# Moving the query stage's normalisations, transposes and two small bias steps in a two-layer attention and feed-forward kernel

## The chip, the cores and the metric

The kernel runs on one core of one Trainium2 chip. A core has engines that run side by side and meet only at semaphores: TensorE (PE in the profile; its weight loads are PEld), VectorE (DVE), ScalarE (ACT), GpSimd (POOL) and SyncE (SP), which here issues most of the transfers between memory and the on-chip buffer. The metric is device microseconds for the whole program; each time given for the kernel is a median over runs.

## The reference: what is computed

Inputs are `x` (8 batches of 112 tokens, width 512), a context `ctx` (8 batches of 375 rows, width 512) and masks of valid context rows, all float32. Two layers follow each other, each an attention over the context and a feed-forward net of hidden size 1408, and all four parts add their result to `x`:

```
x = x + xattn0(layernorm(x), ctx, mask)          # one head, softmax(x ctx^T / sqrt(512)) ctx
x = x + ffn0(layernorm(x), w1, w2, w3)           # quantized: activations to 8 bits, weights to -1, 0, 1
x = x + xattn1(layernorm(x), ctx, mask, Wq, bq, Wk, bk, Wv, bv, Wo, bo, ln_gamma, ln_beta, residual_scale)
x = x + ffn1(layernorm(x), wq_gate, s_gate, wq_up, s_up, wq_down, s_down)
```

The change touches the second attention, cut to what matters here (16 heads of 32):

```
q = hs @ Wq.T + bq;  k = at @ Wk.T + bk;  v = at @ Wv.T + bv        # hs = layernorm(x), at = ctx
scores = clip(q k^T / sqrt(32), -50, 50), masked;  probs = softmax(scores)
ctx = probs @ v
delta = clip(residual_scale, 0, 0.3) * (ctx @ Wo.T + bo)
return layernorm(delta) * ln_gamma + ln_beta
```

Since the probabilities of a row sum to 1, the bias of the values reaches the output as a constant, `bv @ Wo.T`. The kernel computes the values without it and adds that constant to `bo`.

## The kernel before, in words

**Tiles.** The 896 tokens are 7 tiles of 128 rows (`xs[0]` to `xs[6]`, slices of `tokens`). Products run over tokens in two groups: group 0 is tiles 0 to 3, group 1 tiles 4 to 6 (`GROUPS`). "Turning" a tile is transposing it on TensorE against an identity matrix, into PSUM, from where ScalarE or VectorE copies it.

**Stages.** First the attention of layer 0, one batch at a time (about 0 to 100 us), then its feed-forward net, one tile at a time (to about 218 us), the queries of layer 1 (to 244 us), its attention in 8 batches of 3 context chunks (to some 413 us) and its feed-forward net. Through all of these until near the end, `fill(n)` takes the next n steps of `key_value_steps`, which compute keys and values of layer 1 (L193, L202) as work for TensorE in between.

**What sets the order.** TensorE and SP run in the order in which the program is written. Inside `written` (from the middle of layer 0's attention to L694) and in the attention of layer 1 (`work2`) all five engines do. Between the two, which is the stretch of the queries, and in the first microseconds, a planner orders VectorE, ScalarE and POOL by its own estimate of durations. It can also place such free instructions among those of `written`. A buffer is handed on when all readers of its former tile are done.

**Preparing the queries.** For each tile, `write2` (L217) normalises it on VectorE into a tile `d` of two buffers (L644 for tiles 0 to 3, L156 for tiles 4 to 6). `transpose2` (L221) turns it with four transposes (L226) into a PSUM tile `s` of a pool of four buffers. Then ScalarE writes a rounded high part (L229); the function that `transpose2` returns, the tile's "end", has VectorE write the low part (L232, which reads PSUM) and a difference (L233). `turn_down0(6)` turns the last tile of layer 0's net: 11 transposes (L349) into two more buffers of `s`, each copied by ScalarE (L351). In the kernel before, tiles 0 and 1 are turned, then for each of them its end and the write of tile 2 or 3 follow, then `turn_down0(6)`, the turning of tiles 2 and 3, their ends, one step of `fill` (L202) and the last down product (L579, added to `xs[6]` in L581).

**The queries.** `queries(g)` (L724) goes over four chunks of 128 columns: 8 products (L732, L734) of high and low parts, 4 more (L738) of the difference into a second PSUM tile `less`, from the `s` pool; ScalarE adds the queries' bias `bq` (L740) and VectorE subtracts `less` (L742) into `qT`. Ahead of them POOL issues loads (L163): bq, wo, bo, gamma, beta, rs, the mask m, later sg and su. L711 and L713 work on rs. `normaliser` computes a tile's statistics (L143, L144) and a chain of small VectorE operations (L152, L121 to L133): "ln2b" for tiles 4 and 5, "ln2c" for tile 6. On TensorE, two chunks of group 0 come first, then tiles 4, 5 and 6 are turned with one chunk after each as long as there are some (two), then group 1's four chunks.

**The values' bias.** `fold_bias` (L745) is a generator of two steps: four VectorE operations over Wo, scaled by bv (L748, L750), and a product with ones (L754) added to bo (L755). It is run around group 1's queries. Its result is first used when a tile is projected (L804), in batch 2.

**The attention of layer 1.** For each batch b and context chunk c: scores on TensorE (L900), clipped on VectorE (L905), exponentials on ScalarE (L906), a step of `fill`, and the products with the values and the row sums (L926, L921) of the chunk before. POOL adds up exponentials (L892) and converts weights (L877).

Of the kernel before, what the change touches and what calls it, by code (L numbers as in the profile page):

```python
# [23 lines left out]
F32 = mybir.dt.float32  # L24
# [11 lines left out]
P = 128  # L36
B, T, D = 8, 112, 512
KC = D // P
# [4 lines left out]
NT = B * T // P  # L43
# [27 lines left out]
def two_layers(ctx: ExitStack, tc: tile.TileContext, x, ctxT, ctxN, mask0, mask1, w1, w2, w3,  # L71
               wq, wk, wv, wo, bq, bk, bv, bo, gamma, beta, rscale,
               wg, sg, wu, su, wd, sd, out):
    nc = tc.nc
# [5 lines left out]
    kvp = kvs.enter_context(tc.tile_pool(name="kvp", bufs=1))  # L80
# [16 lines left out]
    xs = [tokens[:, i, :] for i in range(NT)]  # L97
# [49 lines left out]
    def normaliser(srcs, name):  # L147

        mv = moments(srcs, name)
        r = srcs[0].shape[0]  # L150
        ve = small[-1].tile([P, len(srcs)], F32, name=f"{name}_ve", bufs=1)[:r]
        nc.vector.tensor_scalar_add(ve, mv[:, :, 1], LN_EPS)  # L152
        rstd = rsqrt(ve, name)

        def write(h, j):
            nc.vector.tensor_scalar(h, srcs[j], mv[:, j, 0:1], rstd[:, j:j + 1],  # L156
                                    ALU.subtract, ALU.mult)
        return write


    def load(pool, src, shape, name, queue=nc.sync, dtype=F32):
        t = pool.tile(shape, dtype, name=name)
        queue.dma_start(out=t, in_=src)  # L163
        return t

    bk_s = kvp.tile([P, KC], F32, name="bk")
    bv_s = kvp.tile([P, KC], F32, name="bv")
    wk_s = kvp.tile([P, KC, D], F32, name="wk")
    wv_s = kvp.tile([P, KC, D], F32, name="wv")
# [40 lines left out]
    def fill(n=1):  # L210
        for _ in range(n):
            next(kv_steps, None)
# [4 lines left out]
    def write2(i, write, j, pool):  # L217
        h2[i] = pool.tile([P, D], F32, name="d", bufs=2)
        write(h2[i], j)

    def transpose2(i, psum):  # L221

        g = 0 if i < GROUPS[0][1] else 1
        pt = psum.tile([P, KC, P], F32, name="s")
        for kc in range(KC):
            nc.tensor.transpose(pt[:, kc, :], h2[i][:, kc * P:(kc + 1) * P], ident)  # L226
        j = i - GROUPS[g][0]
        high, low, diff = (t[:, :, j * P:(j + 1) * P] for t in h2T[g])
        nc.scalar.activation(high, pt, AF.Identity, scale=LESS)  # L229

        def end():
            nc.vector.tensor_sub(low, pt, high.bitcast(F32))  # L232
            nc.vector.scalar_tensor_tensor(diff, high.bitcast(F32), SPLIT, low.bitcast(F32),  # L233
                                           ALU.mult, ALU.subtract)
        return end


    with tc.tile_pool(name="w0", bufs=1, side="right") as w0p, \
# [119 lines left out]
        with tc.tile_pool(name="work0", bufs=2, side="right") as work0, \  # L358
                tc.tile_pool(name="last0", bufs=1, side="right") as last0:

            m0 = load(work0, mask0, [B, S2], "m0", nc.scalar, U8)
            nc.scalar.dma_start(out=bk_s, in_=bk)
            x0 = []
            LN0 = (0, 1, 4)
            cNs, normal, h0, hT0, s0, eT0 = {}, {}, {}, {}, {}, {}
# [162 lines left out]
        with tc.tile_pool(name="work1", bufs=2, side="right") as work1:  # L528
# [43 lines left out]
            def turn_down0(i):  # L572
                q3[i] = transposed_h(q3[i][0], H, "q3", work1), q3[i][1]
# [45 lines left out]
            for i in range(2, NT):  # L619
# [61 lines left out]
                elif i == 5:  # L681
                    wq_diff = []
                    h2T_diff = difference()
                    h2T[0] = h2T_high, difference(), h2T_diff
            ends = [transpose2(k, ps_s) for k in range(2)]
            for k in range(2):
                ends[k]()
                write2(k + 2, normal2, k + 2, work1)
            turn_down0(NT - 1)
            ends = [transpose2(k, ps_s) for k in range(2, 4)]  # L690
            for end in ends:
                end()
            fill(1)
            written.close()  # L694
# [4 lines left out]
    tailp = ctx.enter_context(tc.tile_pool(name="tailp", bufs=1, side="right"))  # L699

    ps_s = ctx.enter_context(tc.tile_pool(name="ps_s1", bufs=4, space=PSUM))
    ps_mm = ctx.enter_context(tc.tile_pool(name="ps_mm1", bufs=2, space=PSUM))
    kv_psum[0] = ps_mm

    bq_s = load(tailp, bq, [P, KC], "bq", nc.gpsimd)
    wo_s = load(tailp, wo, [P, KC, D], "wo", nc.gpsimd)
    bo_s = load(tailp, bo.to_broadcast([P, D]), [P, D], "bo", nc.gpsimd)
    gamma_s = load(tailp, gamma.to_broadcast([P, D]), [P, D], "gamma", nc.gpsimd)
# [15 lines left out]
    def queries(g):  # L724
        i0, i1 = GROUPS[g]
        cols = slice(i0 * P, i1 * P)
        high, low, diff = h2T[g]
        for dc in range(KC):
            of = slice(dc * P, (dc + 1) * P)
            ps = ps_mm.tile([P, 512], F32, name="mm")[:, :(i1 - i0) * P]  # L730
            for kc in range(KC):
                nc.tensor.matmul(ps, lhsT=wq_high[:, kc, of], rhs=high[:, kc, :],  # L732
                                 start=(kc == 0), stop=False)
                nc.tensor.matmul(ps, lhsT=wq_low[:, kc, of], rhs=low[:, kc, :],  # L734
                                 start=False, stop=(kc == KC - 1))
            less = ps_s.tile([P, 512], F32, name="s")[:, :(i1 - i0) * P]
            for kc in range(KC):
                nc.tensor.matmul(less, lhsT=wq_diff[kc // 2][:, kc % 2, of], rhs=diff[:, kc, :],  # L738
                                 start=(kc == 0), stop=(kc == KC - 1))
            nc.scalar.activation(qT[:, dc, cols], ps, AF.Identity, bias=bq_s[:, dc:dc + 1],  # L740
                                 scale=1.0 + SPLIT)
            nc.vector.tensor_sub(qT[:, dc, cols], qT[:, dc, cols], less)  # L742
            yield

    def fold_bias():  # L745

        t = tailp.tile([P, D], F32, name="d", bufs=2)
        nc.vector.tensor_scalar_mul(t, wo_s[:, 0, :], bv_s[:, 0:1])  # L748
        for kc in range(1, KC):
            nc.vector.scalar_tensor_tensor(t, wo_s[:, kc, :], bv_s[:, kc:kc + 1], t,  # L750
                                           ALU.mult, ALU.add)
        yield
        ps = ps_mm.tile([P, D], F32, name="mm")
        nc.tensor.matmul(ps, lhsT=ones, rhs=t, start=True, stop=True)  # L754
        nc.vector.tensor_add(bo_s, ps, bo_s)  # L755
        yield

    kv_psum[1] = False
    asking = queries(0)
    next(asking)  # L760
    next(asking)
    with tc.tile_pool(name="g1p", bufs=1, side="right") as g1p:
        h2T[1] = [g1p.tile([P, KC, 384], F32R, name=f"h2T1_{k}") for k in range(3)]
        write = normaliser(xs[4:6], "ln2b")
        for i in range(4, NT):
            if i == NT - 1:
                write = normaliser(xs[i:], "ln2c")
            write2(i, write, i % 2, tailp)
            transpose2(i, ps_s)()
            next(asking, None)  # L770
        folding = fold_bias()
        next(folding)
        for _ in queries(1):
            pass
        next(folding)
    queried.close()
    tail2 = ctx.enter_context(tc.tile_pool(name="tail2", bufs=1, side="right"))

# [67 lines left out]
    with tc.tile_pool(name="work2", bufs=1, side="right") as work2, \  # L846
# [95 lines left out]
        STEPS = [3, 3, 3, 3, 2, 3, 3, 3]  # L942
        ADD_POOL = range(B - 1)
        last, rdens, later = None, {}, []
        counts = list(due.values())
        load_integers(counts.pop(0))
        for b in range(B):
            for c in range(NCK):
                if c == 2 and b in ADD_POOL:
                    add(b)  # L950
                if (b, c) in due:
                    convert_integers()
                    if counts:
                        load_integers(counts.pop(0))
                es = scores(b, c)
                if c == 2 and b not in ADD_POOL:
                    add(b)
                if c < STEPS[b]:
                    fill(1)
                if c == NCK - 1:  # L960
                    sums(*last)
                if (b, c) == (B - 1, NCK - 1):
                    over = tailp.tile([P, 29], F32, name="over")
                    nc.gpsimd.tensor_scalar(over, squares, WIDE, 1.0, ALU.is_gt, ALU.mult)
                if c == 0:
                    while later:
                        later.pop()()
                    if b >= 3:
                        project_end(b - 3)
                elif c == 1 and b >= 1:  # L970
                    divide(b - 1)
                elif c == 2:
                    turned = 3 <= b < 3 + GROUPS[0][1]
                    if turned:
                        write4(b - 3)
                    if b >= 2:
                        project_product(b - 2)
                    if b == B - 1:

                        hits = ps_s.tile([1, 29], F32, name="s")  # L980
                        nc.tensor.matmul(hits, lhsT=ones[:, :1], rhs=over, start=True, stop=True)
                        wide = tailp.tile([1, 1], I32, name="wide")
                        nc.vector.tensor_reduce(wide, hits, AX.X, ALU.max)
                    if b >= 2:
                        project_begin(b - 2)
                    if turned:
                        later.append(transpose4(b - 3, ps_mm, "mm"))
                if last and c < NCK - 1:
                    sums(*last)
                last = b, c, es  # L990
# [187 lines left out]
```

## Time and profile before

| | |
|---|---|
| median of 3 runs | 523.79 us (523.18 to 524.82) |
| the profiled execution | 523.3 us |
| its span, first to last instruction | 521.4 us |
| mean granted TensorE clock | 0.99 of full speed |
| the queries' stage: first L732 to first L900 | 218.42 to 244.04 us |
| data moved | 45.75 MB, mean 88 GB/s |

The page gives for each engine the time in which it was busy. A busy TensorE says that its queue held running products, not at which rate they ran: the granted clock is a row of its own, in tenths of full speed. Other answers list, for each engine, which wait cost how much (total, times, longest), cut the time into stretches with busy time and clock for each, or list the instructions in order of time; there an entry in square brackets is the idle time of the engine just before the instruction and what ended it. Line numbers (L226) are those of the kernel shown above.

### The profile page before, as it was taken

The page shows a single profiled execution, that of the slowest core. Times are in us where ns is not written, and L with a number is a line of the kernel's source. Part 1 is how long each engine was busy: PE and PEld are TensorE (multiplying, and loading weights), DVE is VectorE, ACT ScalarE, POOL GpSimd, SP SyncE. Part 2 cuts the span into 40 slices and gives each one's busy share as a digit, 9 for nine tenths or more (in the row PEclk, how much of TensorE's full clock was granted, in tenths as well). Part 3 has the DMA queues.
Part 4 walks back from the last instruction along what each step waited for, and adds up shares of the span by engine and source line. Part 5 has one row for each costly group of instructions (what it writes and reads, how often), then busy time and mean ns, then how long its engine had stood idle before and what let it go on. Part 6 is the DMA issues. An engine that isn't in the chain of part 4 may idle for free.

```text
span 521.4 us, 8802 instructions
## 1 busy us (share of the span) xinstructions
PE 504.7 (97%) x3380; PEld 317.0 (61%) x3380; DVE 335.7 (64%) x801; ACT 252.6 (48%) x438; POOL 134.8 (26%) x222
## 2 busy tenths in 40 slices
PE   9999999999999998889999999999999999999995
PEld 6445554454554455578655555555555788889983
DVE  3552548767788987784465588997897774434432
ACT  0336746857655656033876266466665224103310
POOL 0000211111011272020542376576762440000000
PEclk9999999999999999898999999999999999999998
DMA  8998795200210100041152111011321000010001
GB/s 232 334 411 345 252 350 189 70 2 0 87 54 1 60 2 0 2 143 52 52 170 64 60 49 44 23 51 38 86 63 52 22 1 1 16 46 20 1 20 45
DMA packets 13231, 45.75 MB, mean 88 GB/s; under 512 B 1969, under 2 KB 3008, under 8 KB 12032
## 3 DMA queue, kind: packets, MB, share of 16 engines
q1 hardware_dynamic: 11744, 41.43, 23.3%
q0 software_dynamic: 1280, 3.70, 2.1%
q8 instruction: 28, 0.46, 0.4%
q14 instruction: 19, 0.16, 0.1%
q10 hardware_dynamic: 160, 0.01, 0.0%
HBM read 41.46 MB, written 1.84 MB: 83 GB/s over the span
## 4 chain that ended last, share of the span: by engine, by line
PE 79%; DVE 12%; POOL 2%; ACT 2%; DMA 2%; issue 2%; DVEq 0%; ACTq 0%; POOLq 0%
PE mm L202 14%; PE s L1026 14%; PE mm L193 12%; PE down L1044 7%; PE mm L539 5%; PE mm L429 4%; PE mm L798 4%; PE s L400 4%; PE s L900 4%; PE num L926 3%; PE den L921 2%; PE mm L579 2%; DVE e L905 2%; DVE e L937 1%; DMA rs<-in_rscale_dram 1%
## 5 line engine op out<-in xcount | busy, mean ns | idle before, releaser
L202 PE MATMUL mm<-wv,cT 128*125 128x512 f32 x192 | 88.7, 606 | 0.0
L193 PE MATMUL mm<-cT,wk 128*128 128x375 f32 x256 | 87.4, 486 | 0.0
L1026 PE MATMUL s<-h4T,w 128*128 128x512 f32 (+1 forms) x352 | 72.6, 367 | 0.2 <-PE num L926 0.2
L905 DVE TENSOR_SCALAR e<-s,upper 125x448 f32<-125x448 f32 x96 | 58.9, 677 | 18.5 <-PE s L900 17.7
L1026 PEld LDWEIGHTS s<-h4T,w 128*128 128x128 f32 x352 | 63.6, 188 | 8.8 <-issue 0.5
L906 ACT ACTIVATE e<-e 125x448 f32<-125x448 f32 x96 | 51.8, 571 | 28.1 <-DVE e L905 27.5
L193 PEld LDWEIGHTS mm<-cT,wk 128*128 128x128 f32 x256 | 46.8, 190 | 27.6 <-issue 0.9
L202 PEld LDWEIGHTS mm<-wv,cT 128*125 128x125 f32 x192 | 35.0, 190 | 38.8 <-issue 37.2
L892 POOL TENSOR_TENSOR e<-e,e 125x448 f32<-125x448 f32 x28 | 33.3, 1221 | 14.6 <-PE num L926 14.6
L1044 PE MATMUL down<-w,gu 128*128 128x512 f32 x154 | 36.4, 393 | 0.0
L539 PE MATMUL mm<-w_q,q_qT 128*128 128x512 fp8e4 (+1 forms) x168 | 34.6, 361 | 1.6 <-ACT q_qT L351 1.1
L437 POOL DMA_DIRECT2D tokens<-x x14 | 10.7, 768 | 90.4 <-DVE x L431 62.7
L1034 ACT CAST gu<-gu 128x512 fp32r<-128x512 f32 (+1 forms) x22 | 12.5, 568 | 41.5 <-DVE gu L1032 41.5
L875 ACT ACTIVATE w<-raw,zero_point 128x640 fp32r<-128x640 int32 (+2 forms) x29 | 22.6, 782 | 20.1 <-DMA raw<-in_wd_dram 9.1
L1044 PEld LDWEIGHTS down<-w,gu 128*128 128x128 f32 x154 | 28.7, 188 | 6.1
L568 POOL TENSOR_SCALAR q<-gu 128x704 bf16<-128x704 f32 x14 | 10.8, 790 | 79.9 <-ACT gu L565 79.9
L877 POOL TENSOR_SCALAR w<-raw 128x640 fp32r<-128x640 int32 (+2 forms) x29 | 20.8, 727 | 38.7 <-DVE e L905 25.3
L900 PE MATMUL s<-qT,kv 32*125 32x112 f32 x768 | 28.9, 280 | 0.3
L539 PEld LDWEIGHTS <-q_qT 128*128 128x128 bf16 x168 | 16.3, 98 | 20.4 <-issue 1.9
L1032 DVE SCALAR_TENSOR_TENSOR gu<-s,su,gu 128x512 f32<-128x512 f32 (+1 forms) x22 | 15.0, 684 | 20.8 <-PE s L1026 19.2
L900 PEld LDWEIGHTS s<-qT,kv 32*125 32x125 f32 x768 | 24.2, 183 | 6.5 <-issue 4.9
L798 PE MATMUL mm<-wo,qT 128*128 128x512 f32 x56 | 25.8, 603 | 1.0 <-DVE qT L939 1.0
(237 smaller groups left out, 794.5 us busy)
## 6 DMA issues: line engine op xcount, KB each, us to landing
cT<-in_ctxT_dram SPq DMA_DIRECT2D x13, 750.0 KB, 6.0
raw<-in_w_dram SPq DMA_DIRECT2D x6, 1408.0 KB, 22.3
cN<-in_ctxN_dram SPq DMA_DIRECT2D x8, 768.0 KB, 5.7
raw<-in_wg_dram SPq DMA_DIRECT2D x8, 320.0 KB, 3.0
raw<-in_wu_dram SPq DMA_DIRECT2D x8, 320.0 KB, 2.9
raw<-in_wd_dram SPq DMA_DIRECT2D x8, 320.0 KB, 3.1
out_dram<-d SPq DMA_DIRECT2D x7, 256.0 KB, 2.0
wk<-in_wk_dram SPq DMA_DIRECT2D x4, 256.0 KB, 5.1
```

The source lines that it names most:

```text
L193: nc.tensor.matmul(ps[dc], lhsT=wk_s[:, kc, dc * P:(dc + 1) * P], rhs=cT[:, kc, :], start=(kc == 0), stop=(kc == KC - 1))
L202: nc.tensor.matmul(ps, lhsT=cT[:, kc, c * CK:(c + 1) * CK], rhs=wv_s[:, kc, :], start=(kc == 0), stop=(kc == KC - 1))
L400: nc.tensor.matmul(s, lhsT=hT0[b][:, kc, :], rhs=cTs[b][:, kc, :], start=(kc == 0), stop=False)
L539: nc.tensor.matmul(ps[:, :n], lhsT=qT[:, kc, :], rhs=w[:, kc * H + n0:kc * H + n0 + n], start=(kc == 0), stop=(kc == KC - 1))
L798: nc.tensor.matmul(ps, lhsT=qT[:, kc, i * P:(i + 1) * P], rhs=wo_s[:, kc, :], start=(kc == 0), stop=(kc == KC - 1))
L875: nc.scalar.activation(t, raw, AF.Square, bias=zero_point, accum_out=squares[:, k:k + 1])
L892: add(e, e, e1)
L900: nc.tensor.matmul(ss[r][:, dc, :], lhsT=kT[rows, dc, c * CK:(c + 1) * CK], rhs=qT[rows, dc, b * T:(b + 1) * T], start=True, stop=True)
L905: nc.vector.tensor_scalar(e, ss[r], upper[:, c, b:b + 1], -CLIP, ALU.min, ALU.max)
L906: nc.scalar.activation(e, e, AF.Exp, scale=SC1)
L1026: nc.tensor.matmul(ps[:, :n], lhsT=w[:, c:c + P], rhs=h4T[k][:, kc, :n], start=(kc == 0 and k == 0), stop=(kc == KC - 1 and k == 1))
L1044: nc.tensor.matmul(ps, lhsT=gus[k][:, hc, j * P:(j + 1) * P], rhs=w[:, c:c + D], start=(hc == 0 and k == 0), stop=(hc == HC - 1 and k == 1))
```

## The change

Four edits, none of which changes what is computed:

1. In the preparation of tiles 2 and 3, `write2` of tiles 2 and 3 stands directly behind the turning of tiles 0 and 1. Of the ends only tile 0's is written ahead of `turn_down0(6)`; tiles 1, 2 and 3 have theirs after the turning of tiles 2 and 3.
2. In the queries' stage, tiles 4 and 5 are turned one after the other behind the first two chunks; then follow a chunk, tile 6, the last chunk of group 0, and group 1.
3. `bq` is loaded into a tile of the pool `kvp` by ScalarE's queue at the start of the program, behind `bk`, instead of by POOL ahead of the queries.
4. `fold_bias` runs in batch 0 of layer 1's attention: its VectorE step at chunk 1, its product and addition at chunk 2.

```
     bk_s = kvp.tile([P, KC], F32, name="bk")
+    bq_s = kvp.tile([P, KC], F32, name="bq")
...
             nc.scalar.dma_start(out=bk_s, in_=bk)
+            nc.scalar.dma_start(out=bq_s, in_=bq)
...
-            ends = [transpose2(k, ps_s) for k in range(2)]
+            ends = []
             for k in range(2):
-                ends[k]()
+                ends.append(transpose2(k, ps_s))
                 write2(k + 2, normal2, k + 2, work1)
+            ends[0]()
             turn_down0(NT - 1)
-            ends = [transpose2(k, ps_s) for k in range(2, 4)]
-            for end in ends:
+            for k in range(2, 4):
+                ends.append(transpose2(k, ps_s))
+            for end in ends[1:]:
                 end()
             fill(1)
...
-    bq_s = load(tailp, bq, [P, KC], "bq", nc.gpsimd)
     wo_s = load(tailp, wo, [P, KC, D], "wo", nc.gpsimd)
...
         write = normaliser(xs[4:6], "ln2b")
-        for i in range(4, NT):
-            if i == NT - 1:
-                write = normaliser(xs[i:], "ln2c")
-            write2(i, write, i % 2, tailp)
+        for i in range(4, 6):
+            write2(i, write, i - 4, tailp)
             transpose2(i, ps_s)()
-            next(asking, None)
-        folding = fold_bias()
-        next(folding)
-        for _ in queries(1):
-            pass
-        next(folding)
+        next(asking)
+        write2(6, normaliser(xs[6:], "ln2c"), 0, tailp)
+        transpose2(6, ps_s)()
+        for g in range(2):
+            for _ in asking:
+                pass
+            asking = queries(1)
     queried.close()
...
         last, rdens, later = None, {}, []
+        folding = fold_bias()
...
+                if b == 0 and c > 0:
+                    next(folding)
                 if c == 0:
                     while later:
                         later.pop()()
```

## The prediction

> **What bounds the kernel now.** The profiled execution took 523.3 us, 521.4 of them its span. The page comes first: the busy row and the clock row.
>
> ```profile
> PE 504.7 (97%) x3380; PEld 317.0 (61%) x3380; DVE 335.7 (64%) x801; ACT 252.6 (48%) x438; POOL 134.8 (26%) x222
> PEclk9999999999999999898999999999999999999998
> ```
>
> TensorE is the bound nearly everywhere, so a change pays only where it takes away TensorE idle time, TensorE work or a slow clock. The clock row has two dents, in slices 17 and 19 (13 us each), around 210 and 235 us. The list of what TensorE waited for, longest first, has its largest entry and two others in the same place:
>
> ```profile
> PE s L226 <- DVE d L644: 3.2, 2, 2.0
> ...
> PE mm L734 <- DVE h2T L232: 1.0, 1, 1.0
> ...
> PE mm L732 <- ACT h2T L229: 0.7, 1, 0.7
> ```
>
> To see how clock and waits hang together I cut TensorE's time into stretches of 3.413 us, the length of the dents, counted from the edge of one. Columns: stretch, length, busy time, instructions, granted clock, DMA share, GB/s.
>
> ```profile
> 176.45:179.86 3.41, 2.27 (x12) 1.00 0.68 225
> 179.86:183.27 3.41, 3.41 (x18) 1.00 0.00 0
> ...
> 207.17:210.58 3.41, 0.63 (x4) 1.00 0.00 0
> 210.58:213.99 3.41, 3.25 (x7) 0.50 0.00 0
> ...
> 231.06:234.47 3.41, 1.75 (x8) 1.00 0.00 0
> 234.47:237.89 3.42, 3.42 (x13) 0.50 0.00 0
> ```
>
> Both dents fill exactly one stretch, and each follows a stretch that was 18% or 51% busy. One that was 66% busy (first row) is followed by full clock. So idle time here is paid twice: once itself, once as 1.7 us lost in the next stretch. The timeline shows who is late (start, duration, engine and line):
>
> ```profile
> 206.17 0.78 PE L349 MATMUL s<-ident_h,q 128*128 128x128 bf16 x11
> ...
> 208.27 0.54 DVE L644 TENSOR_SCALAR d<-tokens,mv,ln2a_y 128x512 f32<-128x512 f32 x1
> ...
> 210.74 1.09 PE L226 MATMUL s<-ident,d 128*128 128x128 f32 x4 [1.16 <-DVE d L644]
> ...
> 211.62 4.78 PE L202 MATMUL mm<-wv,cT 128*125 128x512 f32 x8
> ```
> ```profile
> 222.63 1.42 ACT L740 ACTIVATE qT<-mm,bq 128x512 f32<-128x512 f32 x2 [10.17 <-DMA bq<-in_bq_dram]
> ...
> 228.57 0.15 DVE L711 TENSOR_SCALAR rs<-rs 128x1 f32<-128x1 f32 x1 [0.36 <-DMA rs<-in_rscale_dram]
> ...
> 243.09 1.02 PE L754 MATMUL mm<-d,ones 128*128 128x512 f32 x2
> 243.36 0.55 DVE L742 TENSOR_TENSOR qT<-qT,s 128x384 f32<-128x384 f32 x1 [1.56 <-PE s L738]
> ...
> 244.04 0.96 PEld L900 LDWEIGHTS s<-qT,kv 32*125 32x125 f32 x32 [0.76 <-DVE qT L742]
> ```
>
> **Part A: tiles 2 and 3 written earlier.** Before, VectorE finishes tiles 0 and 1 (L232, L233) ahead of each write (L644), so the transposes of tiles 2 and 3 start at 208.95 and 210.74. After, both writes stand first. VectorE is free at 206.28 (the L581 of 205.49 ends then). Tile 0's transposes, which free its buffer, start at 205.29, and four take 0.44 (eight, to the next L349: 0.88), so the first write can go at 206.28. Two writes take 1.00 (the pair at 202.31); L232 of tile 0 follows at about 207.20 and ends at 207.88 (0.68). Tile 2's transposes also need a PSUM buffer. All four are held, by tiles 0 and 1 and the two of turn_down0; the first free are tile 0's after that L232, or turn_down0's first after its copy on ScalarE at about 207.65. I take the later, plus the 0.14 from L644's end to the transposes in the trace: 208.02. Tile 3 takes turn_down0's buffer and follows at once. Two tiles take 0.88, so L202 starts at 208.90, not 211.62: 2.72. Idle falls from 3.17 (2.01 + 1.16) to 1.07, so the stretch is at least 69% busy. That lies above the 66% that kept the clock; then the part of L202 from 211.62 to 213.99 runs at full rate: 2.37 / 2 = 1.19. **A = 3.9 us.** ScalarE's order is unchanged (its two copies end at 208.3, the earliest tile 2 can need it). VectorE's nine busy microseconds from 206.28 to 215.5 keep their sum; the eight L232/L233 now end near 213.3, and the first product that reads the last of them (L734) comes at 215.1. What falls late instead is ln2b's chain of small operations, which tile 4 needs. Its write stood at 219.67 for transposes at 224.08: over 3 us of cover.
>
> **Part B: fifth, sixth, seventh tile turned sooner.** TensorE's order was chunk, chunk, t4, chunk, t5, chunk, t6, then group 1, which waits for t6's ScalarE and VectorE halves: 0.69 + 0.99 idle, and the clock drops. Now it is chunk, chunk, t4, t5, chunk, t6, chunk, group 1. The work up to group 1 is the same, so group 1 can start where t6's four transposes end: 230.44 + 0.35 (t4's, 224.08 to 224.43) = 230.79. Its four chunks take 2.11 each (starts 238.87 and 240.98): 239.23. t6's L229 (0.60), L232 (0.69) and L233 (0.69) make 2.0 us with their starts, and lie under a chunk of 2.8. At the end the scores wait for the last L742: before, from the last L738 at 242.39 to L900 at 244.04 are 1.65, of which 0.70 is L738's own. So L900 starts at 239.23 + 0.95 = 240.18, not 244.04. **B = 3.86 us**, about 1.7 of it idle time, 1.7 clock. In these 3.86 lie the two passes of L754: before, they filled the wait for L742.
>
> **Part C: values' bias in batch 0.** The four VectorE operations cost 0.49 + 3 x 0.75 = 2.74. In batch 0 they stand between the L905 of c=1 (ends 252.36) and of c=2 (starts 255.50): 3.14 free, so nothing. Without that cover each microsecond would delay e of c=2, which has some 4 us (its exponentials end near 258.6, its sums begin at 262.84). The product L754 is two passes, 0.86 in the chain, put where TensorE has no idle time: **+0.86**. L755 then waits for it ahead of the next L905 on VectorE, but those scores come 0.86 later too. Its "mm" buffer is read by 261, five microseconds before its next user.
>
> **Part D: queries' bias at the start.** On POOL one issue goes (0.61, and 0.21 to the next): wo, bo, gamma, beta, rs, the mask, sg and su move up by 0.82. Rs then lands 0.8 sooner against the tile writes, and L740 no longer waits 10.17. On ScalarE's queue one issue of 0.37 (bk's) goes in behind 1.34; behind it ScalarE has nothing before its table load at 5.54. The load is 128 rows of 16 bytes at a time when DMA is full. Bounds: nothing; or, if it holds the queues for as long as bk's and the mask's 160 packets (0.7% of the first 16 us, 0.11 us), 0.1 for the first product that needs wk. I take **+0.1**.
>
> **Sum:** -3.9 - 3.86 + 0.86 + 0.1 = -6.8 us against the profiled 523.3. The median, 523.79, is 0.5 above that execution; the same difference gives **517.0 us**, 1.3% less.
>
> **Row against rule.** The Trainium skill, "TensorE: Matmul & The Clock Gate", section "What's actually happening", has the clock halve after at least one idle window of about 3.4 us, and its section on HAM oscillation asks only for no idle gap above that. The gaps here are at most 2.01 us, so by the page no clock would be won: A is 3.17 - 1.07 = 2.1, B is 3.86 - 1.7 = 2.2, and 517.0 becomes about 520.4. The rows decide, since half-clock stretches do follow stretches 18% and 51% busy; the page's word that the window runs freely, so that its edges may fall elsewhere in another run, is taken into the range.
>
> **Rivals.**
> 1. *Tile 3 gets tile 1's PSUM buffer* (chance 0.12). Then it waits for L232 of tile 1, which now stands behind L232 and L233 of tile 0 and, if the planner puts it in that gap as it did at 206.28, ln2b's statistics: about 209.7. L202 starts near 210.5, the stretch is about 35% busy, and the clock drops after all: A is about 1.0, so 519.9. For it: the order of the code releases that buffer last. Against: turn_down0's are free by 208.3.
> 2. *The clock drops anyway in A* (0.10): the statistics go in ahead of the writes (0.6 more idle), or the window's edges fall badly. A is 2.1 to 2.7: 518.2 to 518.8.
> 3. *VectorE a little late in B* (0.06), by one to three microseconds in front of t6 or group 1: 518 to 520.
> 4. *VectorE held at L711* (0.06), the case that ends slower. VectorE works in order. Before, L711 waited only 0.36 for rs, because it stood behind L742 of the third chunk. If the planner puts it straight behind the tile writes (220.7 in the old clock), VectorE stands until rs lands, now 227.7; then ln2c's chain (4.4 us from L143 to the write, 220.58 to 224.95), L742 and L232 follow. TensorE loses about 1.4 at the third chunk's L738 (no PSUM buffer) and 4.5 before t6, and up to 2 in clock: 7.9 against 6.8 won, so about 524.9. It decides from 6.8 us of stall on, that is only if L711 stands ahead of ln2c's chain. The trace speaks against it.
> 5. *The change doesn't show* (0.06): the planner, whose order on VectorE, ScalarE and POOL changes with the program, gives back elsewhere what A and B bring: 522 to 527.
>
> **Chances and range.** The forecast has 0.60, with 516.2 to 517.8 as its own range (A's buffer 0.3 earlier, 0.1 of part D, half a microsecond of run to run). 0.3% of 523.8 is 1.6 us, about what a measurement of this kernel can tell from no change. The forecast and rivals 1 to 3 are faster by more: 0.88. Rivals 4 and 5 are split, half within 0.3% and half slower: 0.06 each. The range runs from 516.0 to 521.0: it holds the forecast and rivals 1 to 3, and leaves out 4 and 5.
>
> **What would show it.** A: transposes of tile 2 within 1.2 us of turn_down0's end, tile 3's behind them, no half clock near 211. B: no wait of L732 or L734, no half clock near 230, and about 22 us from the first L732 to the first L900, not 25.6. C: two L754 passes between the sums and scores of batch 0, no L905 late. D: L740 waiting for products only, the first L193 within 0.2 us of 5.04. The prediction is wrong if TensorE waits above 1.5 us at the transposes, if VectorE idles for rs above 1 us, or if the clock is halved with TensorE over 66% busy.

## The result and the profile after

The changed kernel takes 517.12 us (median of 4, 517.05 to 517.36) against 523.54 for the kernel before in the same comparison: a ratio of 0.987, with a 95% interval of 0.986 to 0.989, or 6.4 us less. The profiled execution took 517.36 us, its span 515.6. All lines behind an edit have moved by a few: L226, L232, L202, L732, L742, L754, L900, L905, L1044 of before are L227, L233, L203, L735, L745, L757, L902, L907, L1049 here.

The page of the changed kernel, busy and clock rows:

```profile
PE 502.3 (97%) x3380; PEld 315.0 (61%) x3380; DVE 334.3 (65%) x801; ACT 252.4 (49%) x438; POOL 133.9 (26%) x221
PEclk9999999999999999999999999999999999999998
```

Both dents in the clock row are gone; the 8 at the end, behind the last product, is there before and after. From the list of what TensorE waited for (total, times, longest), the two entries that are left in the stages of the change:

```profile
PE s L227 <- DVE h2T L233: 0.8, 1, 0.8
...
PE s L902 <- DVE qT L745: 0.3, 1, 0.3
```

The 3.2 us at the transposes have become 0.8, and the waits inside the queries are gone; 0.3 is new in front of the first scores. The timeline of the changed kernel shows the steps in order (start, duration, engine, line):

```profile
205.41 1.04 PE L227 MATMUL s<-ident,d 128*128 128x128 f32 x8
...
206.28 0.99 DVE L646 TENSOR_SCALAR d<-tokens,mv,ln2a_y 128x512 f32<-128x512 f32 x2
206.28 0.78 PE L350 MATMUL s<-ident_h,q 128*128 128x128 bf16 x11
...
207.19 0.68 DVE L233 TENSOR_TENSOR h2T<-s,h2T_high 128x512 fp32r<-128x512 f32 x1
...
207.88 1.09 PE L227 MATMUL s<-ident,d 128*128 128x128 f32 x8 [0.82 <-DVE h2T L233]
...
208.81 3.60 PE L203 MATMUL mm<-wv,cT 128*125 128x512 f32 x8
...
214.43 0.58 PE L735 MATMUL mm<-h2T_high,wq_high 128*128 128x512 f32 x1
...
223.91 0.14 DVE L714 TENSOR_SCALAR rs<-rs 128x1 f32<-128x1 f32 x1
...
235.56 0.48 PE L902 MATMUL s<-qT,kv 32*125 32x112 f32 x6
...
236.35 1.12 PE L902 MATMUL s<-qT,kv 32*125 32x112 f32 x26 [0.31 <-DVE qT L745]
...
241.03 1.14 PE L902 MATMUL s<-qT,kv 32*125 32x112 f32 x32
...
245.07 2.33 DVE L753 SCALAR_TENSOR_TENSOR d<-wo,bv,d 128x512 f32<-128x512 f32 x3
...
247.79 2.46 DVE L907 TENSOR_SCALAR e<-s,upper 125x448 f32<-125x448 f32 x4 [0.39 <-PE s L902]
...
251.33 1.12 PE L757 MATMUL mm<-d,ones 128*128 128x512 f32 x2
...
252.38 1.14 PE L902 MATMUL s<-qT,kv 32*125 32x112 f32 x32
```

Tile 2's transposes start as tile 0's low part ends (207.87), and tile 3's follow in the same run of eight. VectorE does not stand for rs (L714 has no idle time in front of it). The values' bias fits between two L907, and its product delays the scores of batch 1.

How far the changed kernel is ahead at each milestone, from the two timelines. Those of the kernel before that are not shown above:

```profile
218.42 0.58 PE L732 MATMUL mm<-h2T_high,wq_high 128*128 128x512 f32 x1
...
248.74 1.14 PE L900 MATMUL s<-qT,kv 32*125 32x112 f32 x32
...
259.04 1.14 PE L900 MATMUL s<-qT,kv 32*125 32x112 f32 x32
...
447.83 5.22 PE L1044 MATMUL down<-w,gu 128*128 128x512 f32 x22
```

| | before | after | ahead | gained here |
|---|---|---|---|---|
| first transposes of tile 0 | 205.29 | 205.41 | -0.12 | -0.12 |
| values' step (L202) behind tile 3 | 211.62 | 208.81 | 2.81 | 2.93 |
| first query product (L732) | 218.42 | 214.43 | 3.99 | 1.18 |
| scores of batch 0, chunk 1 | 248.74 | 241.03 | 7.71 | 3.72 |
| scores of batch 1, chunk 0 | 259.04 | 252.38 | 6.66 | -1.05 |
| first down product of the last net (L1044) | 447.83 | 441.38 | 6.45 | -0.21 |
| end of the span | 521.4 | 515.6 | 5.8 | -0.65 |

The last row is a loss that the prediction does not have. The last 66 down products of that net, before:

```profile
499.87 15.28 PE L1044 MATMUL down<-w,gu 128*128 128x512 f32 x66
```

and after:

```profile
493.72 15.55 PE L1049 MATMUL down<-w,gu 128*128 128x512 f32 x66
```

The length of the row by its products is 15.55 / 66 = 0.2356 us, not 15.28 / 66 = 0.2315; over all 154 down products the difference makes about 0.6. The query products of 512 columns show the same: the second chunk of group 0 takes 2.78 us, not 2.73. These are untouched instructions, and TensorE does not wait for anything among them.

### The profile page after: what moved, and what is told of

It is laid out like the page before. It is cut to its first block, busy times and chain, and to the rows that moved or that the text cites. A ratio compares the mean times of both kernels' runs of the same rounds, so it can differ in the third digit from the quotient of the medians.

```text
span 515.6 us, 8804 instructions
## 1 busy us (share of the span) xinstructions
PE 502.3 (97%) x3380; PEld 315.0 (61%) x3380; DVE 334.3 (65%) x801; ACT 252.4 (49%) x438; POOL 133.9 (26%) x221
## 4 chain that ended last, share of the span: by engine, by line
PE 47%; DVE 6%; POOL 2%; DMA 1%; ACT 1%; issue 1%; DVEq 0%; POOLq 0%
PE s L1031 14%; PE mm L203 8%; PE down L1049 7%; PE mm L800 4%; PE s L902 3%; PE num L928 2%; PE mm L194 2%; DVE e L907 2%; PE den L923 2%; DMA raw<-in_wd_dram 1%; PE mm L737 1%; PE mm L735 1%; PE s L741 1%; DVE e L939 1%; POOL ln_t L108 1%
## 5 line engine op out<-in xcount | busy, mean ns | idle before, releaser
L203 PE MATMUL mm<-wv,cT 128*125 128x512 f32 x192 | 87.6, 599 | 0.0
L907 DVE TENSOR_SCALAR e<-s,upper 125x448 f32<-125x448 f32 x96 | 59.0, 676 | 14.7 <-PE s L902 13.9
L203 PEld LDWEIGHTS mm<-wv,cT 128*125 128x125 f32 x192 | 34.5, 187 | 38.0 <-issue 36.4
L1049 PE MATMUL down<-w,gu 128*128 128x512 f32 x154 | 37.0, 396 | 0.0
L1049 PEld LDWEIGHTS down<-w,gu 128*128 128x128 f32 x154 | 28.6, 188 | 6.7
L902 PE MATMUL s<-qT,kv 32*125 32x112 f32 x768 | 29.3, 280 | 0.6 <-DVE qT L745 0.3
L902 PEld LDWEIGHTS s<-qT,kv 32*125 32x125 f32 x768 | 24.5, 183 | 7.1 <-issue 5.6
```

Of the source, the lines that this page charges most:

```text
L203: nc.tensor.matmul(ps, lhsT=cT[:, kc, c * CK:(c + 1) * CK], rhs=wv_s[:, kc, :], start=(kc == 0), stop=(kc == KC - 1))
L902: nc.tensor.matmul(ss[r][:, dc, :], lhsT=kT[rows, dc, c * CK:(c + 1) * CK], rhs=qT[rows, dc, b * T:(b + 1) * T], start=True, stop=True)
L907: nc.vector.tensor_scalar(e, ss[r], upper[:, c, b:b + 1], -CLIP, ALU.min, ALU.max)
L1049: nc.tensor.matmul(ps, lhsT=gus[k][:, hc, j * P:(j + 1) * P], rhs=w[:, c:c + D], start=(hc == 0 and k == 0), stop=(hc == HC - 1 and k == 1))
```

## The experiments

Ratios are against the kernel before, run on the same chip beside each kernel; a gain in us is taken from the ratio.

**Edit 1 alone.**

```
-                ends[k]()
+                ends.append(transpose2(k, ps_s))
                 write2(k + 2, normal2, k + 2, work1)
+            ends[0]()
             turn_down0(NT - 1)
```

> Edit 1 alone on the kernel before (tiles 2 and 3 written ahead). Theory that idle time is paid twice (itself and half a clock stretch): -3.9 us, about 519.7, with the half clock near 211 gone and the one near 235 still there. Rival, only the idle time counts: -2.1, about 521.5.

519.87 us (519.53 to 520.64), ratio 0.992 (0.990 to 0.995): 4.0 us, as the prediction's A. The rival's 2.1 lies outside the interval. The half clock near 211 is gone. TensorE's wait for tile 6's low part in the queries has grown from 1.0 to 1.8, and the half clock there stays. The wait, and the two stretches of 3.41 us (start:end, length, busy, instructions, clock):

```profile
PE mm L736 <- DVE h2T L232: 1.8, 1, 1.8
```
```profile
228.17:231.58 3.41, 1.60 (x10) 1.00 0.00 0
231.59:235.00 3.41, 3.41 (x12) 0.50 0.00 0
```

**Edit 2 alone.**

```
+        for i in range(4, 6):
+            write2(i, write, i - 4, tailp)
+            transpose2(i, ps_s)()
+        next(asking)
+        write2(6, normaliser(xs[6:], "ln2c"), 0, tailp)
+        transpose2(6, ps_s)()
+        for _ in asking:
+            pass
         folding = fold_bias()
         next(folding)
```

> Edit 2 alone: tiles 4 to 6 turned sooner, while the values' bias keeps its place around group 1's queries and the queries' bias its load. Theory paid twice: the product L754 still lies in the wait for the last L742, so -3.9, about 519.7, and up to 0.5 less if the bias's four VectorE operations fall in front of tile 6's low part. Half clock near 235 gone, the one near 211 there. Rival, only the idle time counts: -2.2, about 521.4.

Median 520.35 us, ratio 0.993 (0.990 to 0.996): 3.8 us. But the executions fall into two sets, 518.00 and 518.16, and 520.35, 520.90 and 521.21. The mean granted clock, recorded for each execution, is 0.997 and 0.996 in the first set and 0.993 in the second; the difference is about one stretch of 3.41 us at half speed (0.0033 of the span), though such a stretch costs 1.7 us at most and the sets lie 2.2 to 3.2 apart, so that part of the difference stays open. The profiled execution is the first of these. In the queries it has neither a wait nor a half clock, as expected. At the transposes of tiles 2 and 3 TensorE waits its 3.2 us as in the kernel before, and, against the expectation, no stretch at half clock follows.

Where the stretches lie can be counted. In the other traces with a halved stretch, its start lies a whole number of times 3.4133 us ahead of the drop of the clock behind the last product (in the kernel before 210.57 and 517.77: 90 times). With edit 2 alone that drop lies at 512.62, so there are edges at 205.42, 208.84 and 212.25:

```profile
205.42:208.84 3.42, 1.48 (x19) 1.00 0.00 0
208.84:212.25 3.41, 2.19 (x11) 1.00 0.00 0
```

The wait of 2.0 us and that of 1.2 fall into different stretches, 43% and 64% busy, and neither is followed by half clock. In the kernel before, both fall into one, 18% busy. So the same idle time costs its clock in one execution and not in another.

**Edit 4 alone.** `fold_bias` leaves the queries and runs in batch 0.

```
-        folding = fold_bias()
-        next(folding)
         for _ in queries(1):
             pass
-        next(folding)
...
+                if b == 0 and c > 0:
+                    next(folding)
```

> Edit 4 alone: the values' bias in batch 0, the rest as before. Its product costs what it took in batch 0 of the changed kernel, +1.0, since before it lay in the wait for the last L742. But the four VectorE operations no longer stand in front of tile 6's low part (L232 at 232.41 began 0.74 after its input was there): TensorE's stretch would go from 51% to about 72% busy. Theory paid twice with an edge between 51% and 66%: -0.7 idle, -1.7 clock, so about 522.3. Rival, only the idle time counts: +0.3, about 523.9.

522.96 us (520.51 to 523.77), ratio 0.998 (0.9963 to 0.9996): 1.0 us less, although the step costs TensorE a microsecond in batch 0. The rival would have been slower. The wait for tile 6's low part shrinks as expected and no half clock follows it:

```profile
PE mm L734 <- DVE h2T L232: 0.3, 1, 0.3
```

So part of the gain booked under B is open to this edit too, and the parts don't add up: alone, edits 1, 2 and 4 bring 4.0, 3.8 and 1.0, and edit 3, which comes next, 1.3.

**Edit 3 alone.**

```
+    bq_s = kvp.tile([P, KC], F32, name="bq")
...
+            nc.scalar.dma_start(out=bq_s, in_=bq)
...
-    bq_s = load(tailp, bq, [P, KC], "bq", nc.gpsimd)
```

> Edit 3 alone: the queries' bias loaded at the start by ScalarE's queue, in another pool. As predicted: +0.1 from the start (523.7). Rival, the layout: the two pools' tiles behind it move by a few bytes per partition, and in the changed kernel the 154 products of the last down projection run at a spacing of 0.2356 us in place of 0.2315, and the queries' 512-column products likewise: +0.6 to +0.8 more, about 524.4, with the same spacings here.

523.44 us (520.62 to 524.64), ratio 0.9975 (0.996 to 0.999): 1.3 us less, and neither expectation holds. The spacing in the last net is the slow one:

```profile
500.00 15.55 PE L1045 MATMUL down<-w,gu 128*128 128x512 f32 x66
```

Edits 1, 2 and 4 alone have 15.28. But a loss in this net does not come with edit 3 alone. The last 176 gate and up products (384 columns), in the kernel before, with edit 1 alone and with edit 2 alone:

```profile
469.36 30.67 PE L1026 MATMUL s<-h4T,w 128*128 128x384 f32 x176
```
```profile
466.21 31.25 PE L1028 MATMUL s<-h4T,w 128*128 128x384 f32 x176
```
```profile
463.58 31.25 PE L1028 MATMUL s<-h4T,w 128*128 128x384 f32 x176
```

Edits 1 and 2 move no buffer to another pool. From the first down product to the end of the span, the kernel before takes 73.6 us and edit 4 alone too, edits 1 and 2 alone 74.1, edit 3 alone 74.2.

Against the loss stands the clock. In the profiled execution it is at half speed from 209.4 to 216.2 us, two stretches on end, but not in the queries, where the waits are 0.7 + 0.9 in place of 0.7 + 1.0 and fall into two stretches, 80% and 73% busy. The mean clock over the 20 executions is 0.9934, against 0.9916 over the 32 of the kernel before: up to 0.9 us of the 1.3. Why the edit brings fewer halved stretches stays open.

**One end back in front of the writes,** from the changed kernel:

```
-                ends.append(transpose2(k, ps_s))
-                write2(k + 2, normal2, k + 2, work1)
-            ends[0]()
+            ends = [transpose2(k, ps_s) for k in range(2)]
+            ends[0]()
+            for k in range(2):
+                write2(k + 2, normal2, k + 2, work1)
```

> The changed kernel, but the writes of tiles 2 and 3 stand behind tile 0's end (L233, L234) again: one idle stretch of about 2.0 us in place of 0.8 ahead of tile 2's transposes. Theory that the clock's check windows decide: +1.2 in all executions, +2.9 in those in which a window holds most of the idle time; so the executions spread over some 1.7 us between 518.3 and 520.0, where the changed kernel's lie within 0.3. Rival, below 3.4 us of idle time the clock never falls: 518.3 throughout, with no half-clock stretch in the trace.

519.30 us, executions from 518.52 to 519.96, ratio 0.992 (0.991 to 0.993). The trace has one wait of 2.0 us, and after it a stretch at half clock from 209.5 to 212.9:

```profile
PE s L227 <- DVE d L646: 2.0, 1, 2.0
```
```profile
206.08:209.49 3.41, 1.40 (x18) 1.00 0.00 0
209.50:212.91 3.41, 3.41 (x8) 0.50 0.00 0
```

A single wait far below 3.4 us halves the clock, but not in each execution: the three fastest of the six (518.52 to 519.18) have a mean clock of 0.998 or 0.999, which leaves no room for a halved stretch (0.0033), the other three 0.992 to 0.995.

**Every buffer back in its place.**

```
-    bk_s = kvp.tile([P, KC], F32, name="bk")
-    bq_s = kvp.tile([P, KC], F32, name="bq")
+    bkq = kvp.tile([P, 2 * KC], F32, name="bk")
+    bk_s, bq_s = bkq[:, :KC], bkq[:, KC:]
...
+    room = tailp.tile([P, KC], F32, name="room")
+    nc.gpsimd.memset(room, 0.0)
```

> The changed kernel with every buffer where the kernel before had it: bq shares bk's 32 bytes per partition, and a tile of the same size, set to zero by POOL, stands where bq was. Theory that the weights' place costs: moved by 32 bytes, wq_high, wq_low and the last net's gu no longer start at a multiple of 64, and their products run at 0.2356 in place of 0.2315 us; put back, -0.65 in the last down projection and -0.2 in the queries, about 516.3. Rival, the spacing comes from the new order: 517.1.

518.38 us (517.49 to 520.74), ratio 0.991 (0.989 to 0.993), where the changed kernel has 0.987 (0.986 to 0.989): slower. The down products are back at 15.28 us for the 66, but the 176 ahead of them take 31.25 as with edits 1 and 2 alone, and the setting to zero brought a new wait. The timeline of this kernel:

```profile
215.51 0.10 POOL L710 MEMSET room<- 128x4 f32 x1 [9.95 <-DVE ln2b_t L131]
...
218.27 0.61 POOL L163 DMA_DIRECT2D wo<-in_wo_dram  x1 [2.65 <-issue]
...
226.00 0.15 DVE L716 TENSOR_SCALAR rs<-rs 128x1 f32<-128x1 f32 x1 [2.31 <-DMA rs<-in_rscale_dram]
```

POOL's loads start 2.65 us behind the memset, rs lands late, and VectorE stands for it with tile 6's low part behind it; TensorE loses 0.7 there. This is the prediction's rival 4 in small: the mechanism exists, and 2.65 us on POOL's queue set it off.

**The values' bias back around group 1's queries,** from the changed kernel:

```
+        for _ in asking:
+            pass
+        folding = fold_bias()
+        next(folding)
+        for _ in queries(1):
+            pass
+        next(folding)
...
-                if b == 0 and c > 0:
-                    next(folding)
```

> The changed kernel with the values' bias around group 1's queries again: its product L754 behind the last query product and ahead of the first scores, where TensorE waits 0.6 to 0.8 us for the last L742. Theory: batch 0 gets back the 1.06 that the product took there (0.9 to 2.0 us between the sums and the scores), and 0.1 to 0.3 is lost at the queries: about 516.2. Rival, the four VectorE operations hold up tile 6's low part as before: no gain or a loss, 517 to 518.

516.29 us (516.13 to 516.77), ratio 0.986 (0.985 to 0.988), against the expected 516.2. By the ratios (0.9863 against the changed kernel's 0.9874) that is 0.6 us less, within the intervals of both; the traces show it. The product L757 stands at 235.99, the first scores follow at 236.94 with no wait in front of them, and between sums and scores of batch 0 are 0.90 us in place of 1.96. The rival does not show: no wait for tile 6's low part.

**Both together,** and the values' step in front of the transposes of tiles 2 and 3:

```
             turn_down0(NT - 1)
+            ends[1]()
+            fill(1)
             for k in range(2, 4):
                 ends.append(transpose2(k, ps_s))
-            for end in ends[1:]:
+            for end in ends[2:]:
                 end()
-            fill(1)
```

> Both of these together, and the step of keys and values (eight products L203, 3.6 us) ahead of the transposes of tiles 2 and 3 in place of behind them, with tile 1's end in front of it: it covers the 0.8 us that are left of the wait for tile 0's low part. Sum: -0.8 - 0.85 - 0.9 = -2.5, about 514.6. Rival: the ends of tiles 2 and 3 then come late for the first query product, 0.5 to 1 us back, about 515.4.

517.01 us (515.71 to 517.09), ratio 0.987 (0.985 to 0.989). The wait in front of tile 2 is gone, but POOL stood 2.7 us behind the memset again, and TensorE waited 1.0 for tile 6's low part: a miss by 2.4 us against the expected 514.6, with the cause seen when every buffer went back to its place.

**The same two with the tile set to zero by VectorE,** beside the changed kernel once more:

```
-    nc.gpsimd.memset(room, 0.0)
+    nc.vector.memset(room, 0.0)
```

> The changed kernel once more, beside the next two on the same chip: 0.987 of the kernel before, and executions within 0.5 us of each other, because no check window of the clock holds enough idle time.

517.19 us (516.77 to 517.48), ratio 0.988 (0.986 to 0.989).

> As the run that put every buffer back where it was, but the filling tile is set to zero by VectorE. In that run POOL stood 2.65 us between its setting to zero and its first load, rs landed later, VectorE stood 2.31 for it and TensorE 0.7 behind that. Theory: without that, only the weights' places are left: -0.65 -0.2, so 0.85 us below the changed kernel beside it. Rival: the places don't pay, same time as the changed kernel.

517.24 us (516.30 to 517.49): no gain over the kernel beside it. The profile, of the fastest of the four, does have the old spacing,

```profile
492.89 15.28 PE L1051 MATMUL down<-w,gu 128*128 128x512 f32 x66
```

and its 176 products ahead of them take 30.67; from the first down product to the end are 73.7 us against 74.2 beside it, and the span is 514.5 against 515.2. But four executions that lie 1.2 us apart cannot show 0.65, and with the same places the kernel with the memset on POOL had 31.25 for the 176. In all fourteen traces the down products ran at the old spacing where the buffers lie in the old place and at a slower one where they don't; but the place does not settle what the whole net takes, and that it pays in the median is not shown.

> As the run with all three together, with the filling tile set to zero by VectorE. Sum of its parts against the changed kernel: -0.85 for the places, -0.8 for the values' bias behind the query products, -0.8 for the rest of the wait ahead of tile 2: -2.4 us. Rival: the ends of tiles 2 and 3, now later, hold up the first query products, and VectorE's four operations of the bias tile 6's low part: -1.2 or less.

515.15 us (515.05 to 515.97), ratio 0.984 (0.983 to 0.986), 2.0 us below the changed kernel beside it. No wait for the transposes or in the queries is left among TensorE's. This is the fastest version, although its last net takes 74.2 us from the first down product to the end (15.28 for the 66, 31.25 for the 176), as beside it: nothing of the gain is made there.

**Another place for the last net's buffers,** the kernel before with 64 bytes more in front:

```
+    room = tailp.tile([P, 4 * KC], F32, name="room")
+    nc.vector.memset(room, 0.0)
```

> The kernel before with a tile of 64 bytes per partition more, which moves the last net's gu by 64 bytes. Theory that a start at a multiple of 64 is what counts: the last down projection's spacing stays 0.2315 us. Rival, any move from its old place costs: 0.2356.

It ran once, so its 525.93 us is only a single time (the wait for tile 6's low part had grown to 1.8 us, and the clock was halved twice). The spacing:

```profile
502.24 15.50 PE L1046 MATMUL down<-w,gu 128*128 128x512 f32 x66
```

15.50 / 66 = 0.2348: nearly as slow as a move by 32 bytes, and the 176 ahead of them take 31.14. The theory that a start at a multiple of 64 is what counts falls. What sets these spacings stays open.

## Why the prediction was right, step by step

- **A, 3.9 us.** Right in size and in both terms: 2.93 measured for 2.72, and 1.18 for 1.19. With one end put back, a wait of 2.0 brought the half clock back. The PSUM buffers went as assumed, so rival 1 (tile 1's buffer) and rival 2 (statistics ahead of the writes) did not come. Tile 2 started at once behind tile 0's low part; the 0.14 put in between was not there. Edit 1 alone gave 4.0.
- **B, 3.86.** 3.72 measured. Group 1 starts straight behind group 0, with no wait in front of tile 6 or group 1 (rival 3). The first scores start 21.1 us behind the first query product, 0.6 sooner than forecast, as six of the 32 score passes did not wait for the last L745; the others stood 0.3 for it. Four chunks of group 0 at 2.78 in place of 2.73 are about the difference from 3.86.
- **C, +0.86.** 1.05 measured. TensorE did not stand in front of the product. The 0.86 counts its two passes alone; in the trace before, 0.95 lie between the start of the product and that of the scores behind it (243.09 to 244.04), and the last 0.1 goes with a weight load that came late:

```profile
251.33 0.30 PEld L757 LDWEIGHTS mm<-d,ones 128*128 128x128 f32 x2 [0.17 <-ACT kv L197]
```

  VectorE's operations were hidden, as counted. The prediction saw that the product had lain in the wait for L742, and left it at a cost; put back, it left 0.90 between sums and scores in place of 1.96.
- **D, +0.1.** The bias's load itself is not to be seen: the transposes behind the first products start between 15.34 and 16.23 us in nine profiles with it, between 15.55 and 16.34 in five without, and the first product that reads wk starts at 5.01, not 5.04. What the sum lacks is another term: it has nothing for untouched instructions. They cost 0.65 in the last net and 0.2 in the queries. The slower down products came in each trace with moved buffers, as edit 3 moves what is allocated behind its 16 bytes; but edits 1 and 2 alone lose 0.5 in the same net without a move, and with edit 4 alone the second query chunk takes 2.79 us, so this is not the price of D alone. With this term the sum is -6.0.
- **The number.** The profiled executions, from which the sum was worked out, differ by 5.8 in span where 6.8 was forecast; the medians differ by 6.4. That 517.0 lies only 0.1 below the measured 517.12 is in part luck.
- **Row against rule.** The rows were the better guide: after stretches of 41% (one end back in front) and 47% (edit 1 alone) the clock was halved, with no wait above 2.0 us. But I took the clock terms as certain and they are not: in the profiled execution of edit 2 alone, 3.2 us of idle time cost no clock. What the Trainium skill ("TensorE: Matmul & The Clock Gate", section "What's actually happening") says of a window that runs freely agrees with the edges, which lie 3.4133 us apart within a trace and elsewhere in each, and so decide whether two waits fall into one stretch or two. But no single limit on the busy share fits all traces: 43% left the clock at full with edit 2 alone, 47% and 51% did not elsewhere. What else counts stays open. That the halved stretches differ between executions fits the scatter: the kernel before spreads over 3.8 us in 32 executions with mean clocks of 0.986 to 0.995, the changed one over 0.7 in eight with 0.996 to 0.999.
- **Rival 4**, VectorE held at rs, did not come with this change, where rs landed in time. With POOL 2.65 us later it did, at a price of 0.7.

## What to carry to other kernels

Look at a stall together with the clock in the 3.4 us behind it: where TensorE is the bound, a wait of one or two microseconds can cost as much again, in some executions and not in others, and a change that removes it narrows the scatter too. Work for TensorE that has no fixed place belongs in a wait that will remain; ask of a moved step what it covered. Compare the durations of untouched instructions as well, above all when a buffer changes pools: here they moved by 0.6 us, with and without such a move.

## What had not been expected of the hardware

- The spacing of products is not fixed by their shape. The 128x512 down products of the last net ran at 0.2315 us in all eight traces with the buffers in the old place, at 0.2356 in the five with a move by 32 bytes per partition and 0.2348 with one by 64. The 176 products of 384 columns ahead of them took 30.67 or 31.25 us with the buffers in the old place.
- A halved clock can outlast a stretch that would not have halved it: in the profile of edit 3 alone the second of these stretches is 66% busy, and the third is still at half speed. At full clock 66% had left it at full.

```profile
205.97:209.38 3.41, 1.40 (x18) 1.00 0.00 0
209.39:212.79 3.40, 2.24 (x7) 0.50 0.00 0
212.80:216.21 3.41, 3.41 (x5) 0.50 0.00 0
```

- POOL took 2.65 and 2.71 us from the end of a memset of 0.10 us to the start of its next load, where its loads otherwise follow each other by 0.5 to 0.8. With the memset on VectorE, POOL's first load started 2.4 us sooner (215.87, not 218.27).
